# Queries of the second self attention by sets of seven products, with scores and transposes issued as one step

## The chip, the cores and the metric

The kernel runs on one core of a Trainium2 chip. A core has five engines that run side by side, each with an instruction queue of its own: TensorE (PE in the profile, with its weight loads as PEld), VectorE (DVE), ScalarE (ACT), GpSimd (POOL) and SyncE (SP), which here only issues DMA transfers. The metric is device time in microseconds (us) of one execution, and the time of a kernel is the median of its runs.

## The reference

A pre-LN decoder of two layers, all in float32, on x of 8 x 112 x 512 (8 sequences of 112 tokens, model width 512), with a context of 8 x 375 x 128. Each layer is

```
x = x + SelfAttention(LN(x))
x = x + CrossAttention(LN(x), context)
x = x + FFN(LN(x))
```

The two layers differ in kind. The part that matters here is the second layer's self attention: 16 heads of width 128 in four groups of four, each group with one key and one value head (grouped queries), rotary position on queries and keys, no bias, and a window mask of 128 positions that leaves out nothing at 112 tokens:

```
q = x @ Wq.T    (512 -> 16 heads x 128)      k, v = x @ Wk.T, x @ Wv.T   (512 -> 4 heads x 128)
q, k = q * cos + rotate_half(q) * sin, k * cos + rotate_half(k) * sin
out  = softmax(q k^T / sqrt(128)) v          then   x = x + out @ Wo.T
```

Ahead of it stands the first layer's FFN with ternary weights, behind it the second layer's cross attention and an FFN of experts.

## The kernel before

Tokens lie in 7 tiles of 128 (NT), and for the projections in two halves hf of 448 tokens (HT, four sequences). The normalised activations of a half, transposed, are xT[hf], 128 x 4 x 448. A float32 matmul shows in the trace as two PE instructions (passes).

**Turns.** The second self attention runs in eight turns (g, hf): group 0 with hf 0 and 1, then groups 1, 2, 3. A turn has two units of two sequences each. `prepare(n)` makes a turn's key and four query heads: `roped` (L621) multiplies with 4 matmuls of 128 x 448 (`accumulate`, L244), copies the result out of PSUM (raw_q or raw_k, L630 by VectorE; the first layer uses ScalarE at L632), starts two DMA transfers by SP that swap the halves of the head (turned_q, L637), multiplies raw by cos on GpSimd (L639) and turned by sin on VectorE (L640), and adds the two on GpSimd (L641). PSUM tiles of these products come from `mm`, which has two buffers.

**A unit.** `scores` (L695) gives eight 112 x 112 products; `softmax` takes the maximum on VectorE (nmax, L466), eight exponentials with sums on ScalarE (L469), a reciprocal on VectorE (L472) and the multiplication on GpSimd (L476). `probs_transposed` has two steps: four PE transposes each (ppt, L487) and a copy to pT (L488) by VectorE. `contexts` (L714) multiplies with the values and ScalarE copies the result to oT (L719).

**Outputs.** In groups 0 to 2 two token tiles at a time go through `out_pair`, which computes a 2 x 2 block product with seven block products instead of eight (`sevens`, L276 to L307, matmuls at L286). It needs sums of blocks: os (of oT) by `block_sums` (VectorE L253 and L257, GpSimd L256 and L258) and wos (of the weights) by `block_differences` (VectorE L267, L271, L272, GpSimd L270). After each product a *put* reads the PSUM bank: L771 copies, L768 adds, both on VectorE; x is completed by L782 and L785 on GpSimd. Several products accumulate on a bank that an earlier put has to read first. Single tiles go through `project_out` (L442, L446, L447).

**What sets the order.** `weave(main, filler)` lays filler steps between main steps in proportion to written costs. In `pipeline` (L493) the main steps of unit u of turn n are: scores of the following unit, the transposes of this one (0.45 each), its contexts; fillers are the next turn's `prepare` steps and the outputs, in proportion. Each engine's instructions then run in the order in which they were issued. The opening is at L1308: while the ternary FFN's last products (`fall`, L1245, with ScalarE top_h L1142 and VectorE rest_h L1143) run, `weave` inserts the first values, the tile normalisation of the coming attention (transposes `turned_tile`, L390 and copy L394) and the key and query steps of turn 0.

## Time and profile before

| what | value |
| --- | --- |
| runs shown | 1812.27, 1814.44, 1814.93 us (median 1814.44) |
| the profiled execution's own time | 1811.55 us |
| its span in the profile | 1809.5 us |
| mean granted TensorE clock | 0.998 of full speed |
| second self attention in the trace | about 884 to 1195 us of the span |
| in 884 to 1195 us: PE, VectorE, ScalarE, GpSimd busy | 305.2, 149.9, 66.2, 165.3 of 311 us |

The profile's page gives busy time of each engine, the chain of work that ended last, and groups of instructions by line. The trace behind it can be asked for one engine's waits, for the timeline of a stretch, or for busy time by windows with the granted clock. In a timeline row come the start in us, the duration in us, the engine, line and operation, out<-in, the shape, and in brackets the idle time before and what ended it.

### The profile page before, as it was taken

The page shows a single profiled execution, that of the slowest core. Times are in us where ns is not written, and L with a number is a line of the kernel's source. Part 1 is how long each engine was busy: PE and PEld are TensorE (multiplying, and loading weights), DVE is VectorE, ACT ScalarE, POOL GpSimd, SP SyncE. Part 2 cuts the span into 40 slices and gives each one's busy share as a digit, 9 for nine tenths or more (in the row PEclk, how much of TensorE's full clock was granted, in tenths as well). Part 3 has the DMA queues.
Part 4 walks back from the last instruction along what each step waited for, and adds up shares of the span by engine and source line. Part 5 has one row for each costly group of instructions (what it writes and reads, how often), then busy time and mean ns, then how long its engine had stood idle before and what let it go on. Part 6 is the DMA issues. An engine that isn't in the chain of part 4 may idle for free.

```text
span 1809.5 us, 20342 instructions
## 1 busy us (share of the span) xinstructions
PE 1762.9 (97%) x7150; PEld 989.6 (55%) x7150; DVE 952.1 (53%) x1692; ACT 627.8 (35%) x1906; POOL 770.7 (43%) x673
## 2 busy tenths in 40 slices
PE   8999999999999999999999999999999999999998
PEld 4455544555554555567655666655655444554444
DVE  4555666645353544786543555535765444444444
ACT  2444444554333433375321122136733111041110
POOL 3455555355555550000125666621363354434543
PEclk9999999999999999999999999999999999999999
DMA  6131422143233212011221221220011212011111
GB/s 243 27 119 54 151 82 75 75 152 110 53 79 108 59 53 93 24 71 47 76 60 36 82 73 41 44 86 1 2 44 50 73 62 81 24 51 55 63 34 41
DMA packets 40430, 124.50 MB, mean 69 GB/s; under 512 B 7333, under 2 KB 20701, under 8 KB 32905
## 3 DMA queue, kind: packets, MB, share of 16 engines
q1 hardware_dynamic: 33192, 93.73, 16.2%
q0 software_dynamic: 6848, 29.36, 5.4%
q8 instruction: 56, 0.92, 0.2%
q14 instruction: 46, 0.37, 0.1%
q10 hardware_dynamic: 288, 0.12, 0.0%
HBM read 94.56 MB, written 10.28 MB: 58 GB/s over the span
## 4 chain that ended last, share of the span: by engine, by line
PE 80%; DVE 8%; POOL 4%; DMA 3%; ACT 3%; issue 1%; SPq 1%; ACTq 0%; POOLq 0%; DVEq 0%
PE pr_q L244 10%; PE pf L244 5%; PE po_x L1004 4%; PE pb_dn L1550 4%; PE pv L244 3%; PE po_at L442 3%; PE ps L695 3%; PE po_at L446 3%; PE pr_k L244 3%; PE po_x L442 2%; PE po L714 2%; PE po_x L446 2%; PE pb_up L1550 2%; PE pa_dn L1550 2%; PE pq_x L244 2%; PE pg_dn L1550 2%
## 5 line engine op out<-in xcount | busy, mean ns | idle before, releaser
L244 PE MATMUL pr_q<-xT_at,wq 128*128 128x448 f32 x512 | 204.1, 543 | 0.0
L244 PEld LDWEIGHTS pr_q<-xT_at,wq 128*128 128x128 f32 x512 | 93.9, 190 | 84.3 <-issue 81.2
L469 ACT ACTIVATE p<-p,nmax 112x113 f32<-112x113 f32 x256 | 95.8, 376 | 109.7 <-DVE nmax L466 108.8
L476 POOL TENSOR_TENSOR p<-p,total 112x896 f32<-112x896 f32 (+1 forms) x56 | 85.3, 1529 | 94.9 <-DVE total L472 87.6
L1733 POOL TENSOR_TENSOR h<-silu,h 128x448 f32<-128x448 f32 x64 | 73.9, 1158 | 111.0 <-ACT silu L1731 110.8
L244 PE MATMUL pf<-h,sw 128*128 128x448 f32 x256 | 105.9, 540 | 0.0
L1127 POOL TENSOR_SCALAR tl<-tr,ternary_bounds 128x512 f32<-128x512 f32 x32 | 51.7, 1615 | 122.2 <-DMA tr<-in_c_w_dram 122.2
L974 DVE TENSOR_REDUCE nmax_x<-ps_x 112x2 f32<-112x750 f32 x64 | 57.2, 934 | 79.5 <-PE ps_x L968 79.5
L639 POOL TENSOR_TENSOR qT<-raw_q,tables 128x448 f32<-128x448 f32 x64 | 85.9, 1348 | 27.9 <-DVE raw_q L630 20.4
L641 POOL TENSOR_TENSOR qT<-qT,turned_q 128x448 f32<-128x448 f32 x64 | 75.5, 1183 | 50.4 <-DVE turned_q L640 41.6
L1735 DVE TENSOR_TENSOR h<-h,share 128x448 f32<-128x448 f32 x48 | 41.7, 875 | 105.0 <-POOL h L1733 105.0
L1004 PE MATMUL po_x<-pT_x,kv 125*128 125x448 f32 x192 | 89.2, 549 | 1.3 <-DVE pT_x L999 1.0
L976 ACT ACTIVATE p_x<-ps_x,nmax_x 112x375 f32<-112x375 f32 x124 | 69.7, 574 | 38.2 <-DVE nmax_x L974 38.1
L1550 PE MATMUL pb_dn<-h,sums_dn 128*128 128x448 f32 x192 | 80.2, 540 | 1.0 <-DVE xT_ff L1774 0.5
L1731 ACT ACTIVATE silu<-pf,cols 128x448 f32<-128x448 f32 x64 | 40.5, 633 | 115.6 <-PE pf L244 115.5
L488 DVE COPY pT<-ppt 112x448 f32<-112x448 f32 x96 | 57.1, 617 | 42.5 <-PE ppt L487 42.4
L469 ACT ACTIVATE p<-ps,nmax 112x112 f32<-112x112 f32 x128 | 43.2, 363 | 102.1 <-DVE nmax L466 102.1
L442 PE MATMUL po_at<-wo,oT 128*128 128x512 f32 x152 | 74.3, 611 | 0.0
L244 PEld LDWEIGHTS pf<-h,sw 128*128 128x128 f32 x256 | 48.5, 190 | 46.6 <-issue 40.5
L446 PE MATMUL po_at<-wo,oT 128*128 128x512 f32 x152 | 71.4, 592 | 0.0
L719 ACT COPY oT<-po 128x448 f32<-128x448 f32 x64 | 31.9, 525 | 104.8 <-PE po L714 104.8
L476 POOL TENSOR_TENSOR p_e<-p_e,total_e 112x896 f32<-112x896 f32 x16 | 26.9, 1682 | 96.5 <-DVE total_e L472 72.2
(357 smaller groups left out, 3942.5 us busy)
## 6 DMA issues: line engine op xcount, KB each, us to landing
tw<-in_c_w_dram SPq DMA_DIRECT2D x16, 512.0 KB
tr<-in_c_w_dram POOLq DMA_DIRECT2D x32, 256.0 KB, 3.9
signs<-tl POOLq DMA_DIRECT2D x32, 256.0 KB, 2.9
fup<-in_f_up_dram SPq DMA_DIRECT2D x8, 1024.0 KB
fdn<-in_f_dn_dram SPq DMA_DIRECT2D x8, 1024.0 KB
turned_q<-raw_q SPq DMA_DIRECT2D x128, 56.0 KB
turned_q<-raw_q SPq DMA_DIRECT2D x64, 112.0 KB
share<-gated SPq DMA_DIRECT2D x12, 448.0 KB
```

The source lines that it names most:

```text
L244: nc.tensor.matmul(ps, lhsT, rhs, start=(k == 0), stop=(k == len(pairs) - 1))
L442: nc.tensor.matmul(ps[0], lhsT, rhs, start=(c == 0), stop=False)
L446: nc.tensor.matmul(ps[0], lhsT, rhs, start=False, stop=(c == len(pairs) - 1))
L469: nc.scalar.activation(p[:, h, :], src[:, h, :], AF.Exp, bias=nmax[:, h : h + 1], accum_out=total[:, h : h + 1])
L476: spread[:] = [nc.gpsimd.tensor_tensor(p[:, at, :T], p[:, at, :T], total[:, at], ALU.mult).ins]
L639: nc.gpsimd.tensor_tensor(by_batch(dst), by_batch(raw), cos, ALU.mult)
L641: nc.gpsimd.tensor_tensor(dst, dst, turned, ALU.add)
L974: nc.vector.tensor_reduce(nmax, ps[:T, :, :L], AX.X, ALU.max, negate=True)
L976: e = nc.scalar.activation(p[:, 2 * j + s, :], ps[:T, s, :L], AF.Exp, bias=nmax[:, s : s + 1], accum_out=total[:, 2 * j + s : 2 * j + s + 1],)
L1004: nc.tensor.matmul(po[0][:, : 4 * T], kv[:, b, c, :], pTs[c], start=(c == 0), stop=(c == NLC - 1))
L1550: nc.tensor.matmul(bank[n], lhsT, rhs, start=(k == 0 and n in (1, 6, 7)), stop=(k == len(pairs) - 1), skip_group_check=True,)
L1733: nc.gpsimd.tensor_tensor(to, s, at["h1"][:, c, half(hf)], ALU.mult)
```

## The change

Six things change, all in the second layer's self attention.

1. In turns 2 to 7 the four query heads are computed as two pairs, each by `sevens` at 128 x 224: `paired`, with products of weight blocks (two heads wide, two halves of the model width) and token blocks (224 tokens). The sums of weight blocks come from `add_up(g)`, the differences of activation blocks from `differ(hf)`, laid among the steps of earlier turns. Six of seven puts of a pair are on VectorE, one on ScalarE.
2. The last addition of the rotation of the second pair's second query is on VectorE, the others stay on GpSimd.
3. Scores of the next unit and both transposes of this unit are issued as one main step of cost 2.1, so that no filler lies between.
4. The copy of the transposed probabilities is on ScalarE in this layer, and so are the raw copies of the keys and queries of turns 0 and 1.
5. The opening's `weave` lists keys and queries of turn 0 ahead of the second values step.
6. The temporaries os and od of `out_pair` come from the pool of normalised tiles (tag xn, three buffers), since the other pool now holds the sums.

The diff, cut to its core:

```diff
--- before.py
+++ after.py
@@ -476 +476 @@
             spread[:] = [nc.gpsimd.tensor_tensor(p[:, at, :T], p[:, at, :T], total[:, at], ALU.mult).ins]
         return p
 
-    def probs_transposed(pool, p, kept, name):
+    def probs_transposed(pool, p, kept, name, copy=nc.vector.tensor_copy):
 
 
         def turn(k):
@@ -485 +485 @@
             pt = turning(f"ppt_{name}_{k}").rearrange("p (h t) -> p h t", h=4)
             for h in range(4):
                 nc.tensor.transpose(pt[:T, h, :T], p()[:, 4 * k + h, :T], ident[:T, :T])
-            copied[:] = [nc.vector.tensor_copy(kept["pT"][:, 4 * k : 4 * k + 4, :], pt[:T, :, :T]).ins]
+            copied[:] = [copy(kept["pT"][:, 4 * k : 4 * k + 4, :], pt[:T, :, :T]).ins]
 
         return [(0.45, lambda: turn(0)), (0.45, lambda: turn(1))]
 
 
-    def pipeline(turns, units, ahead, prepare, scores, contexts, outputs, extra, begun=None, finale=None, between=False, keys_early=()):
+    def pipeline(turns, units, ahead, prepare, scores, contexts, outputs, extra, begun=None, finale=None, between=False, keys_early=(), grouped=False):
 
 
 
@@ -507 +507 @@
                 coming, own = scored(n * units + u + ahead), contexts(n, u)
                 if between:
                     steps += own[:2] + coming + own[2:]
+                elif grouped and coming:
+                    steps.append((2.1, lambda part=coming + own[:2]: run(part)))
+                    steps += own[2:]
                 else:
                     steps += coming + own
             return steps
@@ -548 +551 @@
         half = width // 2
         turns = [(g, hf) for g in range(G) for hf in range(2)]
         held, matrices = [{} for _ in turns], {}
-        dq, wos = [], {}
+        dq, xs, sums, wos = [], {}, {}, {}
 
...
@@ -606 +609 @@
             if n < 1:
 
                 first, last = (0, 3 if l0 else 2) if n < 0 else (6, 8)
-                return [(3.4, lambda b=b: values(b)) for b in range(first, last)]
+                steps = [(3.4, lambda b=b: values(b)) for b in range(first, last)]
+                if not l0 and n == 0:
+                    more = later(add_up(1) + differ(0))
+                    steps = [*more[:3], steps[0], *more[3:6], steps[1], *more[6:]]
+                return steps
             if not l0:
-                return []
+                g, hf = turns[n]
+                return later(differ(1) if n == 1 else add_up(g + 1) if hf == 0 and g + 1 < G else [])
...
+        def new_raw(name):
+            return top.tile([P, HT], F32, tag="raw", bufs=3, name=f"raw_{name}")
+
         def roped(dst, w, at, xh, bias, which, name):
+
+            ps = mm(f"pr_{name}")
+            accumulate(ps[:, :HT], [(w[:, c, at : at + P], xh[:, c, :]) for c in range(NC)])
+            raw = new_raw(name)
+            if bias is None and name.startswith("k") and xs:
+                nc.vector.tensor_copy(raw, ps[:, :HT])
+            elif bias is None:
+                nc.scalar.copy(raw, ps[:, :HT])
+            else:
+                nc.scalar.activation(raw, ps[:, :HT], AF.Identity, bias=bias)
+            rotated(dst, raw, which, name)
+
+        def differ(hf):
+
+            b = xT[hf].rearrange("p (h k) (s t) -> p h k s t", h=2, s=2)
+
+            def new():
+                xs[hf] = dq[0].tile([P, 4, 2, HT // 2], F32, tag=f"xs{hf}", bufs=1, name=f"xs_{layer}_{hf}")
+
+            return block_differences(
+                (nc.vector, nc.gpsimd), new, lambda k: xs[hf][:, k],
+                b[:, 0, :, 0], b[:, 0, :, 1], b[:, 1, :, 0], b[:, 1, :, 1],
+            )
+
+        def add_up(g):
+
+            a = matrices[g][0].rearrange("p (h k) (c m n) -> p h k c m n", h=2, c=2, m=2)
+
+            def new():
+                sums[g] = dq[0].tile([P, 3, 2, 2, P], F32, tag="sums", bufs=1, name=f"sums_{layer}_{g}")
+
+            return block_sums(
+                (nc.vector, nc.gpsimd), new, lambda k: sums[g][:, k],
+                a[:, 0, :, :, 0], a[:, 1, :, :, 0], a[:, 0, :, :, 1], a[:, 1, :, :, 1],
+            )
+
+        def paired(turn, qT, c, nm):
+
+            g, hf = turns[turn]
+
+            raw = [None, None]
+            half_ = HT // 2
+            tok = [slice(0, half_), slice(half_, HT)]
+
+            def products(n):
+                a = matrices[g][0].rearrange("p (h k) (c m n) -> p h k c m n", h=2, c=2, m=2)
+                b = xT[hf].rearrange("p (h k) (s t) -> p h k s t", h=2, s=2)
+                s, t = sums[g], xs[hf]
+                pick = {
+                    1: lambda k: (a[:, 0, k, c, 0], b[:, 0, k, 0]), 2: lambda k: (a[:, 1, k, c, 0], b[:, 1, k, 0]),
+                    3: lambda k: (s[:, 2, k, c], b[:, 1, k, 1]), 4: lambda k: (a[:, 1, k, c, 1], t[:, 3, k]),
+                    5: lambda k: (s[:, 0, k, c], t[:, 0, k]), 6: lambda k: (s[:, 1, k, c], t[:, 1, k]),
+                    7: lambda k: (a[:, 0, k, c, 1], t[:, 2, k]),
+                }
+                return [pick[n](k) for k in range(2)]
+
+            def put(n, ps):
+                if n == 1:
+                    raw[:] = [new_raw(f"q_{nm}_{2 * c + m}") for m in range(2)]
+                r0, r1 = raw
+                add = lambda to, of: nc.vector.tensor_tensor(to, of, ps, ALU.add)
+                if n == 1:
+                    nc.vector.tensor_copy(r0[:, tok[1]], ps)
+                elif n == 6:
+                    add(r1[:, tok[0]], r0[:, tok[1]])
+                elif n == 2:
+                    nc.scalar.copy(r0[:, tok[0]], ps)
+                elif n == 5:
+                    add(r1[:, tok[1]], r1[:, tok[0]])
+                elif n == 7:
+                    add(r1[:, tok[1]], r1[:, tok[1]])
+                elif n == 3:
+                    add(r0[:, tok[1]], r1[:, tok[0]])
+                    rotated(qT[:, 2 * c, :], r0, "q", f"q_{nm}_{2 * c}")
+                else:
+                    add(r1[:, tok[0]], r1[:, tok[0]])
+                    rotated(qT[:, 2 * c + 1, :], r1, "q", f"q_{nm}_{2 * c + 1}", nc.vector if c else nc.gpsimd)
+
+            first, second = sevens(products, put, half_, f"q_{nm}_{c}", c == 1)
+            return [(2.3, first), (3.0, second)]
+
+        def rotated(dst, raw, which, name, last=nc.gpsimd):
 
             cos, sin = (
                 const(f"{n}{which}{layer}").unsqueeze(1).to_broadcast([P, HB, T]) for n in ("cos", "sin")
             )
-            ps = mm(f"pr_{name}")
-            accumulate(ps[:, :HT], [(w[:, c, at : at + P], xh[:, c, :]) for c in range(NC)])
-            raw = top.tile([P, HT], F32, tag="raw", bufs=3, name=f"raw_{name}")
-            if bias is None:
-                nc.vector.tensor_copy(raw, ps[:, :HT])
-            else:
-                nc.scalar.activation(raw, ps[:, :HT], AF.Identity, bias=bias)
-
             turned = top.tile([P, HT], F32, tag="turned", bufs=3, name=f"turned_{name}")
             for at in range(0, P, half):
                 other = at ^ half
@@ -638 +723 @@
             by_batch = lambda t: t.rearrange("p (b t) -> p b t", b=HB)
             nc.gpsimd.tensor_tensor(by_batch(dst), by_batch(raw), cos, ALU.mult)
             nc.vector.tensor_tensor(by_batch(turned), by_batch(turned), sin, ALU.mult)
-            nc.gpsimd.tensor_tensor(dst, dst, turned, ALU.add)
+            last.tensor_tensor(dst, dst, turned, ALU.add)
 
...
-            more = later(lay(g - 1)) if not l0 and n and hf == 0 else []
-            for c in range(4):
-                steps += more[c : c + 1]
-                steps.append((3.0, lambda c=c: roped(
-                    qT[:, c, :], wq, c * P, xT[hf], col("bq", 4 * g + c) if l0 else None, "q",
-                    f"q_{nm}_{c}",
-                )))
+            if l0 or n < 2:
+                for c in range(4):
+                    steps.append((3.0, lambda c=c: roped(
+                        qT[:, c, :], wq, c * P, xT[hf], col("bq", 4 * g + c) if l0 else None, "q",
+                        f"q_{nm}_{c}",
+                    )))
+            else:
+                more = [step for c in range(2) for step in paired(n, qT, c, nm)]
+                if hf == 0:
+                    more = [step for pair in zip(more, later(lay(g - 1))) for step in pair]
+                steps += more
...
-            return probs_transposed(late, lambda: held[n]["p", u], kept, nm) + [(0.8 if l0 else 1.5, add, True)]
+            copy = nc.vector.tensor_copy if l0 else nc.scalar.copy
+            return probs_transposed(late, lambda: held[n]["p", u], kept, nm, copy) + [(0.8 if l0 else 1.5, add, True)]
 
...
@@ -742 +832 @@
 
             def add_up():
                 def new():
-                    s.append(dq[0].tile([P, 3, 2, P], F32, tag="os", bufs=1, name=f"os_{nm}"))
+                    pair = [npool.tile([P, D], F32, tag="xn", bufs=3, name=f"os_{nm}_{k}") for k in range(2)]
+                    d.append(pair[1][:, D // 2 :])
+                    pair = [t.rearrange("p (s c n) -> p s c n", s=2, c=2) for t in pair]
+                    s.extend([pair[0][:, 0], pair[0][:, 1], pair[1][:, 0]])
 
                 for step in block_sums(
-                    (nc.vector, nc.gpsimd), new, lambda k: s[0][:, k],
+                    (nc.vector, nc.gpsimd), new, lambda k: s[k],
                     a[:, 0, :, tok(0)], a[:, 1, :, tok(0)], a[:, 0, :, tok(1)], a[:, 1, :, tok(1)],
                 ):
                     step()
 
...
             def put(n, ps):
                 if n == 1:
-                    d.append(dq[0].tile([P, 3, D // 2], F32, tag="od", bufs=1, name=f"od_{nm}"))
-                d1, d2, d3 = (d[0][:, m] for m in range(3))
+                    d.append(npool.tile([P, D], F32, tag="xn", bufs=3, name=f"od_{nm}"))
+                d1, d2, d3 = d[0], d[1][:, : D // 2], d[1][:, D // 2 :]
...
+                        x[:, k + 1, :], x[:, k + 1, :], d[1], ALU.add
                     )
 
             first, second = sevens(products, put, D // 2, nm)
@@ -827 +920 @@
             pipeline(
                 turns, HB if l0 else HB // 2, 2 if l0 else 1, prepare, scores, contexts, outputs, extra,
                 begun=None if l0 else 0, finale=finale, between=l0,
-                keys_early=(2, 4) if l0 else (),
+                keys_early=(2, 4) if l0 else (), grouped=not l0,
             )
             if l0:
                 pool.release()
@@ -1305 +1398 @@
                     opening, following = self_attention(1, cross_attention_1, (nc.gpsimd, behind), xT)
 
             keys, values = opening[:5], opening[5:]
-            weave(main, values[:1] + third[1:] + values[1:] + keys[:-1] + more[:1] + keys[-1:] + more[1:])
+            weave(main, values[:1] + third[1:] + keys + more[:1] + values[1:] + more[1:])
             tpool.release()
             wpool2.release()
             following()
```

More of the change, by code (lines that the diff above doesn't have):

```diff
@@ L754, in products @@
                 b = matrices[g][1].rearrange("p (h k) (s n) -> p h k s n", h=2, s=2)
-                t, v = wos[g], s[0]
+                t, v = wos[g], s
                 pick = {
                     1: lambda c: (a[:, 0, c, tok(0)], b[:, 0, c, 0]), 2: lambda c: (a[:, 1, c, tok(0)], b[:, 1, c, 0]),
-                    3: lambda c: (v[:, 2, c], b[:, 1, c, 1]), 4: lambda c: (a[:, 1, c, tok(1)], t[:, 2, c]),
-                    5: lambda c: (v[:, 0, c], t[:, 0, c]), 6: lambda c: (v[:, 1, c], t[:, 1, c]),
+                    3: lambda c: (v[2][:, c], b[:, 1, c, 1]), 4: lambda c: (a[:, 1, c, tok(1)], t[:, 2, c]),
+                    5: lambda c: (v[0][:, c], t[:, 0, c]), 6: lambda c: (v[1][:, c], t[:, 1, c]),
                     7: lambda c: (a[:, 0, c, tok(1)], b[:, 0, c, 1]),
@@ L785, in put @@
                     nc.gpsimd.tensor_tensor(
-                        x[:, k + 1, :], x[:, k + 1, :], d[0][:, 1:].rearrange("p a b -> p (a b)"), ALU.add
+                        x[:, k + 1, :], x[:, k + 1, :], d[1], ALU.add
                     )
```

## Prediction

> **What bounds the kernel now.** I read the shares of busy time first, then the chain of work that ended last, then the waits of TensorE in the stretch of the second self attention (880 to 1215 us), then single stretches of its timeline. From the page of before, busy time and chain:
> ```profile
> PE 1762.9 (97%) x7150; PEld 989.6 (55%) x7150; DVE 952.1 (53%) x1692; ACT 627.8 (35%) x1906; POOL 770.7 (43%) x673
> ...
> PE 80%; DVE 8%; POOL 4%; DMA 3%; ACT 3%; issue 1%; SPq 1%; ACTq 0%; POOLq 0%; DVEq 0%
> ```
> PE is busy 97% and is 80% of the chain, so time goes with PE's passes and its idle gaps. Another engine counts only where PE waits for it. The waits of PE in that stretch (line, releaser, total, times, longest):
> ```profile
> PE ps L695 <- POOL qT L641: 2.3, 1, 2.3
> PE px_at_False L286 <- DVE od_at_False L771: 1.5, 3, 0.5
> ```
> One is the opening, the other recurs in the output sets of three turns. The rest of the list is below 1 us a line. So a gain must come from fewer passes, and a loss from new waits.
>
> **Passes removed.** Turns 2 to 7 compute four heads of queries. Before: 4 x 4 matmuls, which the trace shows as two passes each, 8 per head, 0.376 us from start to start at 448 wide: 32 passes, 12.03 us a turn. After: 2 pairs x 7 products x 2 x 2 passes = 56 passes at 224. No row has 224 wide; rows of 112 (scores, 16 passes in 1.57 us, 0.098 each) and of 256 bound it. The 256-wide sets, PE's timeline near 1004 us:
> ```profile
> 1003.74 1.03 PE L286 MATMUL py_at_True<-wo,os_at_True 128*128 128x256 f32 x4
> 1004.60 1.03 PE L286 MATMUL pz_at_True<-wos,oT 128*128 128x256 f32 x4
> ```
> First column start, second duration: 0.86 us for four passes, 0.216 each. Between 0.098 and 0.216 the line through both gives 0.190 at 224: 56 x 0.190 = 10.6 us, a gain of 1.42 a turn, **8.5 us over six turns**. Bounds: 0.216 gives 12.1 us and no gain; no reason is seen for less than 0.188, half of 0.376.
>
> **What the sets add around PE.** A product that accumulates into a bank starts only after the put of the earlier product has read it. The 256-wide put is 0.42 us and the 448 copy 0.62, so a 224 put is about 0.38; PE to DVE is about 0.2, DVE to PE 0.05. Four passes of 0.19 last 0.76, so one put fits (0.63), and a put with anything ahead of it on DVE does not. From the orders of both kernels:
> - raw_k's copy (0.62) is ahead of the first put: 0.13 a turn. The turned_k multiply (0.62) is ahead of a put of the first pair: 0.2.
> - Output set in front of the scores: turned_q3 and, in hf 0 turns, a sum of 0.44 stand ahead of a put: 0.33 (hf 1), 0.6 (hf 0). Output set behind the scores (hf 0 alone): two sums ahead of a put, 0.3 to 0.65, I take 0.45; but transposes now lie between its first products and the scores' maximum, which takes away that list's second row, 0.5 and 0.1 of unhidden weight load per turn.
> - hf 1: 0.2 for more puts beside sums of 512, and 0 to 0.4, taken 0.2, where the transposes follow scores directly and 7.3 us of work covers a chain of about 7.
>
> Sum: three hf 0 turns -1.42 + 0.13 + 0.2 + 0.6 + 0.45 - 0.62 = -0.66 each; hf 1 turns -1.42 + 0.13 + 0.2 + 0.33 + 0.2 + 0.2 = -0.36 twice, and -0.56 in the last, which has no sums. **Six turns: -3.3.** With no new stall it is -8.5 - 1.9 = -10.4; with 0.9 more a turn (below) +2.1.
>
> **Moved copies.** The transposed probabilities (DVE 0.61) go to ScalarE, where the like copy of oT is 0.53. 32 x 0.61 = 19.6 us leaves DVE, which gets 12 puts of 0.38 (4.6) for four copies of 0.62 (2.5) a turn, six turns: 12.4, and some twelve sums and differences of about 0.7, 8.4; eight raw query copies of turns 0 and 1 (5.0) leave it too. So DVE's load hardly moves. ScalarE's eight exponentials (2.8 us) may stand ahead of a copy; what covers it is the two to four products (over 2 us) between transposes and contexts. Cost 0; without cover about 1 us a unit. The last query add of each turn moves from GpSimd (1.14) to DVE, behind three puts: the chain from the last product to scores is 0.2 + 0.38 + 3.0 (a raw copy ends at 995.67, its turned multiply starts at 998.68) + 0.63 + 0.42 + 0.7 to 1.3 = 5.3 to 5.9, covered by the set of 7 x 0.865 = 6.05. Slack 0.1 to 0.8. The rotation's two SP issues per head stay as many; nothing is moved past them. The stores os and od only change pools: 0 (cover: three buffers).
>
> **The opening.** Keys and the first turn's queries are issued earlier, so that the last query has some 10 us of PE work behind it. PE and windows of before (sum columns: busy PE, load, DVE, ACT, POOL, granted clock, DMA share, GB/s):
> ```profile
> 926.43 1.34 PE L695 MATMUL ps<-kT,qT 128*112 128x112 f32 x12
> 930.07 3.84 PE L695 MATMUL ps<-kT,qT 128*112 128x112 f32 x20 [2.30 <-POOL qT L641]
> ```
> ```profile
> 930.00:932.00 2.00, 1.93 (x10) 1.93 (x11) 1.41 (x2) 0.09 (x1) 0.02 (x1) 0.54 0.00 0
> 932.00:934.00 2.00, 2.00 (x13) 1.93 (x12) 0.76 (x3) 1.71 (x11) 0.00 (x0) 0.61 0.04 8
> 934.00:936.00 2.00, 2.00 (x6) 0.81 (x5) 1.04 (x1) 2.00 (x13) 0.00 (x0) 1.00 0.00 0
> ```
> After an idle of 2.30 us the clock is 0.54 and 0.61, then 1.00: twenty passes took 3.84 instead of 20 x 0.098 = 1.97, so 1.87 more. The 2.30 + 1.87 = 4.17 go. But scores and both transposes are now one step, also in this first step, with nothing between: the transposes of unit 0 follow unit 1's scores (1.57 us). Before, value products (pv, 8 passes of 0.43, 3.4 us each) lay there. The chain of unit 0, timeline of VectorE, ScalarE and GpSimd of before:
> ```profile
> 931.16 1.09 DVE L466 TENSOR_REDUCE nmax<-ps 112x8 f32<-112x896 f32 x1 [0.59 <-PE ps L695]
> ...
> 938.26 3.32 POOL L476 TENSOR_TENSOR p<-p,total 112x896 f32<-112x896 f32 x2 [8.24 <-DVE total L472]
> ```
> 0.2 + 1.09 + eight exponentials 2.8 (932.29 to 935.07) + 0.1 + reciprocal 0.2 + half of 3.32, 1.66 + 0.1 = 6.2: idle 6.2 - 1.57 = 4.6 at least. In the new order VectorE has seven more operations between this maximum and its reciprocal (a sum of 512, unit 1's maximum 1.09, a tile's norm 0.54, two differences of 448, two of 512). The chain is then 1.3 + 0.66 + 1.09 + 0.54 + 4 x 0.66 + 0.2 + 1.76, some 8.2: idle 6.6. The trace has 1.33 and 1.32 us on average for such differences (L272, L271, 512 wide, 3 each), against 0.66 to 0.68 for the first; five at that price add 3.3: idle 9.9. I take 7.0, nearer the free row, since GpSimd is doing little there. The clock after so long an idle: 1.7 of extra time, between 0.9 and 2.6 (half and one and a half windows of the 3.4 us over which the record held 0.5). Opening: 7.0 + 1.7 - 4.17 = **+4.5** (from 4.6 + 0.9 - 4.17 = +1.3 to 9.9 + 2.6 - 4.17 = +8.3). ScalarE's copies of the raw queries, ahead of a step of the FFN that is still running, cost it +0.5 (0 to 1). The first wait in cross attention (pt_xa, 0.5) may go, since its DVE copy is no longer queued: -0.3.
>
> The Trainium skill, "TensorE: Matmul & The Clock Gate", section "Part 1: The HAM clock gate", says the clock falls to half after an idle window of about 3.4 us and returns after a busy one, and that these windows run free. By it the longer idle is certain to throttle, while the 2.30 us of the trace that did so would not alone fill a window; its sum is 3.4 x 0.5 = 1.7 of lost time, an estimate that leaves the opening at +4.5 too, and a stall under 1 us in the turns costs no clock. The skill also speaks against the change's order, "SBUF — State Buffer", section "Who interferes with whom": a VectorE operation with two SBUF inputs is locked out by a GpSimd one that reads SBUF. The rows agree in part (os sums of L257 took 0.42 us on average in some places and 0.83 in others). By this rule the upper end, idle 9.9, would hold, and the whole sum would be +4.3 instead of +1.4.
>
> **Sum.** +4.5 - 3.3 + 0.5 - 0.3 = +1.4 us. Against its own execution: 1811.55 (span 1809.5 and 2.05 around it, left as it is) becomes 1812.95. That execution is 2.9 under the median 1814.44 of the runs shown, which becomes **1815.8**.
>
> **Rivals.**
> (a) Full gain: puts hide, the unit 0 chain is as short as its rows. Six turns -7.5, opening +1.5, rest 0: -6, 1808.4. For it: DVE is only 53% busy. Against: puts are in order behind it.
> (b) Slower: DVE in order decides. If a rotation transfer lands so late that the turned multiply starts more than 3.0 us after its copy, the turned multiply holds the put behind it and PE waits in the products that accumulate; the first head's multiply has no slack beyond the contexts' 1.5 us, the last head's chain 0.1 to 0.8. From about 1 us of lateness it costs 0.9 a turn, 5.4 in all: 1821.2; the opening's upper end of +8.3, 3.8 above the value taken, gives 1819.6. For it: one such multiply in the trace waited 2.47 us for its DMA; the chain has DVE at 8%. Against: passes between are many.
> (c) The sets don't shorten the passes: at 0.216 a turn takes 12.1 instead of 10.6, 8.9 in all: 1824.7. Against: 0.098 at 112 wide, so weight loads don't set 0.19.
>
> **How the numbers follow.** The smallest difference that a measurement of this kernel can tell is about 0.2%, 3.6 us. Forecast 0.50 (1811 to 1818); (a) 0.14; (b) 0.31; (c) 0.05. The range takes the forecast, most of (a) and (b): 1809.5 to 1821.5. Faster takes (a), 0.14, and a rim of the forecast, 0.01; slower takes (b) without its lower rim, 0.29, with (c), 0.05: 0.34.
>
> **What would show it.** Right: the wait of scores for qT (2.3) gone, one wait of the transposes of unit 0 for GpSimd's probabilities of 5 to 10 us with a low clock after it; 224-wide passes at 0.19; waits of L286 on DVE puts of about 1 us a turn. Wrong: opening idle under 4 us, puts that hold PE over 2 us a turn, or a pass at 0.21.

## The result and the profile after

The changed kernel takes 1820.49 us (median of 5 runs, 1817.65 to 1822.79), the kernel before 1813.16 us over 5 runs: ratio 1.0041, 95% interval 1.0028 to 1.0054. That is slower by 7.3 us, 5.1 to 9.8 by the interval. The predicted 1815.8 was 4.7 us short, and as a difference it was 5.9 us short: +1.4 was forecast, +7.3 measured, since the three runs shown ahead of the prediction have a median 1.3 us above that of all five. The range to 1821.5 took the time in, but a difference within the noise was given the largest chance; slower, which came true, had 0.34.

Busy time and the head of the chain of the changed kernel, from its page:

```profile
PE 1761.9 (97%) x7294; PEld 1013.6 (56%) x7294; DVE 958.8 (53%) x1716; ACT 651.2 (36%) x1960; POOL 774.5 (43%) x675
...
PE 79%; DVE 9%; POOL 3%; ACT 3%; DMA 2%; issue 2%; SPq 1%; DVEq 0%; ACTq 0%; POOLq 0%
```

PE has 144 more passes, each shorter, and is busy 1.0 us less in a span that is 7.5 us longer. So most of the time was lost in gaps. The waits of PE in the stretch of the second self attention, 880 to 1225 us (line, releaser, total, times, longest):

```profile
PE ppt L487 <- POOL p L476: 7.7, 3, 7.4
PE pz_at_True L286 <- DVE od_at_True L861: 4.0, 6, 0.9
PE px_at_True L286 <- DVE os_at_True L864: 0.9, 2, 0.4
...
PE py_q L286 <- DVE raw_q L693: 0.7, 1, 0.7
```

The two rows shown of before are gone. In their place stand one long wait of the first transposes and many short ones of accumulating products for VectorE.

The same PE instruction can be looked up in both traces, so each stretch is a difference of two start times:

| stretch (both profiled executions) | before | after | difference |
| --- | --- | --- | --- |
| first value product to first scores | 49.92 | 50.18 | +0.3 |
| first scores to key of turn 1, with 0.77 of transposes that now lie ahead of this key taken off | 15.46 | 20.92 | **+5.5** |
| key of turn 1 to cross attention's first product, the 0.77 added | 252.35 | 254.04 | **+1.7** |
| on to the cross attention's first queries | 21.15 | 20.73 | -0.4 |
| from there to the end | 594.12 | 595.85 | +1.7 |

The start of the first row lies 1.2 us earlier after the change, before any changed step runs; with it the sum is the 7.5 us of the spans. The last row is no work of the change: there PE ran eight passes of the expert FFN in 4.89 us that took 3.25 before, since the granted clock was 0.50 from 1350 us on for 3.4 us.

**How large the waits are.** The profile's list leaves out short waits. I therefore also took, for each PE pass of the third row, its start-to-start interval less the free interval of its width (0.376 us at 448, 0.431 at 512, 0.216 at 256, 0.189 at 224, 0.098 at 112). The sum, called the excess here, is 3.4 us before and 13.7 after: 10.3 more, against 8.6 saved by shorter passes. That is the 1.7.

### The profile page after: what moved, and what is told of

It reads as the page before. It is cut to its first block, busy times and chain, and to the rows that moved or that the text cites. A ratio compares the mean times of both kernels' runs of the same rounds, so it can differ in the third digit from the quotient of the medians.

```text
span 1817.0 us, 20787 instructions
## 1 busy us (share of the span) xinstructions
PE 1761.9 (97%) x7294; PEld 1013.6 (56%) x7294; DVE 958.8 (53%) x1716; ACT 651.2 (36%) x1960; POOL 774.5 (43%) x675
## 4 chain that ended last, share of the span: by engine, by line
PE 79%; DVE 9%; POOL 3%; ACT 3%; DMA 2%; issue 2%; SPq 1%; DVEq 0%; ACTq 0%; POOLq 0%
PE pr_q L244 6%; PE pf L244 5%; PE po_x L1097 4%; PE pb_dn L1643 4%; PE po_at L442 3%; PE pv L244 3%; PE po_at L446 3%; PE pr_k L244 3%; PE pq_x L244 3%; PE po_x L442 2%; PE po_x L446 2%; PE pb_up L1643 2%; PE pa_dn L1643 2%; PE ps L784 2%; PE ps_x L1061 2%; PE po L803 2%
## 5 line engine op out<-in xcount | busy, mean ns | idle before, releaser
L244 PE MATMUL pr_q<-xT_at,wq 128*128 128x448 f32 x320 | 127.7, 545 | 0.0
L724 POOL TENSOR_TENSOR qT<-raw_q,tables 128x448 f32<-128x448 f32 x64 | 77.9, 1228 | 28.3 <-ACT raw_q L640 16.6
L244 PEld LDWEIGHTS pr_q<-xT_at,wq 128*128 128x128 f32 x320 | 58.7, 190 | 54.1 <-issue 50.5
L726 POOL TENSOR_TENSOR qT<-qT,turned_q 128x448 f32<-128x448 f32 x58 | 69.2, 1196 | 43.2 <-DVE turned_q L725 36.3
L725 DVE TENSOR_TENSOR turned_q<-turned_q,tables 128x448 f32<-128x448 f32 x64 | 51.8, 809 | 29.0 <-DMA turned_q<-raw_q 28.5
L1088 PEld LDWEIGHTS ppt_x<-consts,p_x 112*125 112x125 f32 x372 | 50.2, 188 | 29.6 <-issue 15.3
L784 PEld LDWEIGHTS ps<-kT,qT 64*112 64x112 f32 (+1 forms) x768 | 55.0, 175 | 13.8 <-issue 8.2
```

The lines of the kernel that those rows point to most:

```text
L244: nc.tensor.matmul(ps, lhsT, rhs, start=(k == 0), stop=(k == len(pairs) - 1))
L724: nc.gpsimd.tensor_tensor(by_batch(dst), by_batch(raw), cos, ALU.mult)
L726: last.tensor_tensor(dst, dst, turned, ALU.add)
L784: nc.tensor.matmul(ps[:T, 4 * k + h, :T], qT[at, h, bcols(b)], kT[at, bcols(b)], start=True, stop=True)
```

## The experiments

Diffs are cut to the lines that matter. Each time is a median beside runs of the kernel before on the same chip; since that one's median moved between 1811.5 and 1812.7 from one set of runs to the next, ratios are the better comparison. "Turns" is the third row of the table above, in the one profiled execution.

| kernel | median us | ratio to before (95%) | turns us | excess us |
| --- | --- | --- | --- | --- |
| before | 1813.16 | 1 | 252.4 | 3.4 |
| changed | 1820.49 | 1.0041 (1.0028 to 1.0054) | 254.0 | 13.7 |
| E1 opening split | 1811.39 | 0.9996 (0.9987 to 1.0005) | 254.0 | 13.6 |
| E2 nothing grouped | 1811.02 | 0.9992 (0.9983 to 1.0000) | 253.6 | 13.2 |
| E3 plain queries | 1807.42 | 0.9972 (0.9962 to 0.9982) | 250.3 | 1.3 |
| E4 late sums | 1811.37 | 0.9996 (0.9987 to 1.0005) | 253.9 | 13.6 |
| E5 early keys alone | 1808.72 | 0.9987 (0.9979 to 0.9996) | 252.3 | 3.4 |
| E6 plain, nothing grouped | 1807.03 | 0.9974 (0.9964 to 0.9984) | 250.1 | 1.1 |
| E7 rotation on GpSimd | 1818.11 | 1.0029 (1.0016 to 1.0042) | 263.3 | 22.9 |
| E8 additions left out | 1804.83 | 0.9961 (0.9950 to 0.9973) | 248.1 | 7.7 |
| E9 early keys, opening grouped | 1818.32 | 1.0037 (1.0023 to 1.0050) | 252.3 | 3.4 |
| E10 additions on VectorE | 1808.46 | 0.9981 (0.9972 to 0.9990) | 250.7 | 10.3 |
| E11 half of the sets | 1805.75 | 0.9967 (0.9955 to 0.9980) | 247.5 | 2.8 |
| E12 two od buffers | 1808.55 | 0.9980 (0.9970 to 0.9989) | 250.1 | 1.2 |

### E1: the opening split

```diff
-                elif grouped and coming:
+                elif grouped and coming and n:
```

> The changed kernel, but in turn 0 scores and transposes are separate main steps again, so that value products lie between them; all else of the change stays. Theory A (the opening's loss is this one grouping): the idle of 7.36 us ahead of the first transposes and about 2.1 us of half clock behind it go, and nothing replaces them, since three value and key products of over 10 us cover a chain of some 10 us: about 9.5 us under the changed kernel, 1811 us. Rival B (the probabilities are late wherever the transposes stand, because sums of weights and activations stand ahead of them on VectorE and GpSimd): the wait shrinks by the products put in between, but 2 to 4 us of idle stay, and with them the low clock: 1815 us. Rival C: the old wait of scores for the rotated query comes back: 1816 us.

Measured 1811.39 us, 9.1 under the changed kernel: theory A. The opening of the changed kernel, PE and then GpSimd:

```profile
925.51 3.31 PE L784 MATMUL ps<-kT,qT 128*112 128x112 f32 x32
936.18 1.74 PE L487 MATMUL ppt<-consts,p 112*112 112x112 f32 x8 [7.36 <-POOL p L476]
937.71 8.37 PE L244 MATMUL pv<-wv,xT_at 128*112 128x512 f32 x16
```

```profile
929.26 4.77 POOL L258 TENSOR_TENSOR sums<-wq,sums 128x512 f32<-128x512 f32 x1 [0.63 <-DVE sums L257]
934.00 3.77 POOL L476 TENSOR_TENSOR p<-p,total 112x896 f32<-112x896 f32 x2
```

All 32 score passes run through in 3.31 us, so the old wait for the rotated query is gone. Then PE stands for 7.36 us, and eight transposes and two value products take some 2.1 us more than at full clock (9.74 us up to the next transposes, against 7.7 at the free intervals above). The windows show it (granted clock is the third number from the end):

```profile
936.00:938.00 2.00, 1.82 (x9) 1.82 (x10) 0.00 (x0) 0.58 (x2) 1.76 (x2) 0.50 0.04 8
938.00:940.00 2.00, 2.00 (x3) 0.65 (x3) 0.00 (x0) 0.49 (x1) 0.00 (x0) 0.50 0.00 0
940.00:942.00 2.00, 2.00 (x5) 0.77 (x4) 0.00 (x0) 0.00 (x0) 0.00 (x0) 0.90 0.00 0
```

With value and key products in between (E1) no wait of the first transposes is left. The excess of the turns stays: the opening and the turns are two losses.

### E2 and E3: grouping or sets

```diff
-                keys_early=(2, 4) if l0 else (), grouped=not l0,
+                keys_early=(2, 4) if l0 else (), grouped=False,
```

> The changed kernel with scores and both transposes as separate main steps in all turns. Theory A (grouping hurts only in the opening; the waits of the turns come from additions that stand ahead of puts on VectorE): within 2 us of the kernel split in turn 0 alone, with the waits of the output sets on VectorE still some 1 us a turn and 0.5 us more in three turns where the transposes no longer lie between an output set's first products. Rival B (grouping packs the work on VectorE and ScalarE into bursts, and makes the waits of the turns): 4 us or more under the kernel split in turn 0 alone.

```diff
-            if l0 or n < 2:
+            if True:
...
-                    more = later(add_up(1) + differ(0))
...
-            if bias is None and name.startswith("k") and xs:
+            if bias is None and name[4] != "0":
```

> As the kernel split in turn 0 alone, but all queries by plain products of 448 and without the sums and differences that only the sets use; raw copies of groups 1 to 3 by VectorE as before the change, transposed probabilities by ScalarE and scores grouped with transposes from turn 1 on. Theory A (the sets save 8.5 us of passes, and their puts and sums bring about as much in waits): within 3 us of the kernel split in turn 0, with the waits of the output sets on VectorE nearly gone. Rival B (the waits come from grouping, from ScalarE's copies or from the pools, and the sets themselves gain): 6 to 9 us over the kernel split in turn 0, with the waits unchanged.

E2 is 0.4 under E1 with overlapping intervals, its excess 13.2: no gain or loss by grouping in the turns is seen. Theory A held, but for the 0.5 us more in three turns, which didn't come (E12 below has the reason). E3 is 4.0 under E1 and its excess 1.3: A's reason held, no wait of the output sets is listed, but A had allowed 3 us. The sets save 8.6 us of passes and bring 12.3 us of waits: they lose 3.7 (254.0 less 250.3).

### E4: late sums

```diff
+        def after_puts(step):
+            with tc.issue_after(last_put[0]) if last_put else nullcontext():
+                step()
...
-                    step()
+                    after_puts(step)
```

> As the kernel split in turn 0 alone, but VectorE issues the sums of oT blocks and of query weight blocks only after the last put of the output set that stands before them in the program. Theory A (those sums, lengthened by GpSimd to 1.3 us each, hold the puts that PE waits for): the waits of the fourth and seventh product of the output sets fall from 1.0 and 1.2 us a turn to under 0.4, 4 to 6 us in all: 1805 to 1807 us, faster than both kernels. Rival B (the turned queries that wait for their transfers hold the puts, and the sums only stand beside them): less than 2 us: 1809 to 1811 us.

Neither gain came: 1811.37 us, excess 13.6. The waits moved: in hf 0 turns the wait of the set's last product fell from 0.87 to 0.53, and that of the third product, 0.45 in two hf 1 turns, went, but the sums then stood ahead of the scores' maximum, and PE met the result there:

```profile
1045.69 1.83 PE L788 MATMUL ps<-kT,qT 128*112 128x112 f32 x16 [1.00 <-ACT p L469]
1047.92 0.98 PE L487 MATMUL ppt<-consts,p 112*112 112x112 f32 x8 [0.40 <-POOL p L476]
```

The time is B's. Theory A as I put it, that these sums alone hold the puts, fell.

### E8 and E10: standstill or queue

```diff
-                    rotated(qT[:, 2 * c, :], r0, "q", f"q_{nm}_{2 * c}")
+                    rotated(qT[:, 2 * c, :], r0, "q", f"q_{nm}_{2 * c}", None)
...
-                    rotated(qT[:, 2 * c + 1, :], r1, "q", f"q_{nm}_{2 * c + 1}", nc.vector if c else nc.gpsimd)
+                    rotated(qT[:, 2 * c + 1, :], r1, "q", f"q_{nm}_{2 * c + 1}", nc.vector if c else None)
```

> As the changed kernel split in turn 0, but GpSimd's last addition of the rotation is left out for the queries of the sets (so three of four query heads of a turn lack their sine part); the additions of VectorE stay. Theory A (a VectorE operation with two SBUF inputs stands still while one of GpSimd's runs: the sum of oT blocks of 1.30 us and the second turned query of 1.2 to 1.5 us do so): both fall to their free durations of 0.44 and 0.62; the wait of the seventh product in the three output sets of hf 0 falls from 0.87 to under 0.3 us, the sum by 3 to 5 us: 1806 to 1809 us. Rival B (these durations have another reason, such as the transfers that land beside them): they stay, and the time within 1 us of 1811.4.

1804.83 us, 1.2 below theory A's range and far from B's. VectorE in an hf 0 turn of E1 (first, with the row of GpSimd's addition beside it) and of E8 (second), at the same place in the output set; the addition on GpSimd is missing in E8:

```profile
999.70 0.41 DVE L861 TENSOR_TENSOR od_at_True<-od_at_True,py_at_True 128x256 f32<-128x256 f32 x1
1000.02 1.30 DVE L253 TENSOR_TENSOR os_at_False<-oT 128x256 f32<-128x256 f32 x1
1001.25 0.61 DVE L725 TENSOR_TENSOR turned_q<-turned_q,tables 128x448 f32<-128x448 f32 x1
1001.78 0.41 DVE L861 TENSOR_TENSOR od_at_True<-od_at_True,pz_at_True 128x256 f32<-128x256 f32 x1
...
999.91 1.13 POOL L726 TENSOR_TENSOR qT<-qT,turned_q 128x448 f32<-128x448 f32 x1 [1.68 <-DVE turned_q L725]
```

```profile
998.43 0.41 DVE L862 TENSOR_TENSOR od_at_True<-od_at_True,py_at_True 128x256 f32<-128x256 f32 x1
998.76 0.42 DVE L253 TENSOR_TENSOR os_at_False<-oT 128x256 f32<-128x256 f32 x1
999.10 0.62 DVE L725 TENSOR_TENSOR turned_q<-turned_q,tables 128x448 f32<-128x448 f32 x1
999.63 0.41 DVE L862 TENSOR_TENSOR od_at_True<-od_at_True,pz_at_True 128x256 f32<-128x256 f32 x1
```

The sum of oT blocks takes 1.30 us beside GpSimd's addition and 0.42 without it; the put behind it (last row) starts 2.08 us after the row above the sum, against 1.20. PE waits for that put: 0.87 in E1, and no wait is listed in E8. The puts themselves, with one operand in PSUM, take 0.41 in both.

By place, of the 5.9 us of excess that E8 takes away 2.6 lie in the output sets of the hf 0 turns (1.14 to 0.26 a turn), 1.7 in the second pairs, 0.4 in the last turn's output set, and 1.1 where transposes follow the scores at the end of two hf 1 turns; that last part is no put: there the transposes no longer wait for GpSimd's probabilities. In the output sets of those two hf 1 turns, the ones with sums of weight blocks, nothing went: 1.6 us a turn in E1 and in E8. There a sum and a turned query still take 1.33 and 1.35 in E8, each beside another operation of GpSimd, a multiplication by cos and GpSimd's own part of the sums (VectorE, then GpSimd):

```profile
1030.11 1.33 DVE L257 TENSOR_TENSOR sums<-sums,wq 128x512 f32<-128x512 f32 x1
1034.40 1.35 DVE L725 TENSOR_TENSOR turned_q<-turned_q,tables 128x448 f32<-128x448 f32 x1
...
1029.44 1.45 POOL L724 TENSOR_TENSOR qT<-raw_q,tables 128x448 f32<-128x448 f32 x1 [5.11 <-DVE raw_q L693]
1033.62 1.65 POOL L258 TENSOR_TENSOR sums<-wq,sums 128x512 f32<-128x512 f32 x1
```

So theory A holds where the addition runs beside VectorE's operation, and its forecast for the turned query fails here, where the neighbour is another. That these neighbours are the cause in the hf 1 turns is read from the rows; no run left them out.

```diff
-                    rotated(qT[:, 2 * c, :], r0, "q", f"q_{nm}_{2 * c}")
+                    rotated(qT[:, 2 * c, :], r0, "q", f"q_{nm}_{2 * c}", nc.vector)
...
-                    rotated(qT[:, 2 * c + 1, :], r1, "q", f"q_{nm}_{2 * c + 1}", nc.vector if c else nc.gpsimd)
+                    rotated(qT[:, 2 * c + 1, :], r1, "q", f"q_{nm}_{2 * c + 1}", nc.vector)
```

> As the changed kernel split in turn 0, with the last addition of the rotation on VectorE for all queries of the sets, nothing left out. Theory A (two things hold the puts: VectorE's queue, and the standstill beside GpSimd): the second turned query falls from 1.2 to 1.5 us to 0.62, but 0.62 of addition stands in its place, so the waits shift and hardly shrink: 1809 to 1813 us. Rival B (the standstill alone makes the waits): 1804 to 1807 us, as with the additions left out.

1808.46 us lies between the two expectations. Within the self attention the turned queries fell from a mean of 0.80 us (changed kernel) to 0.63, the excess from 13.6 (E1) to 10.3. Both causes are real: of the 12.3 us of waits that the sets bring, 5.9 go when GpSimd's additions are left out (E8), and 3.3 of these remain gained when VectorE does them, so that the additions cost 2.6 again on VectorE. Part of these is queue, seen in the hf 0 turns, where the rows nearly have their free durations and 0.46 us a turn are left, against 0.26 in E8; part is a standstill once more, since in two hf 1 turns one of the additions takes 1.35.

### E7: rotation on GpSimd

In the sets `by` and `last` are GpSimd, elsewhere they stay.

```diff
-            nc.vector.tensor_tensor(by_batch(turned), by_batch(turned), sin, ALU.mult)
+            by.tensor_tensor(by_batch(turned), by_batch(turned), sin, ALU.mult)
```

> As the changed kernel split in turn 0, but in the sets GpSimd does the multiplication of the turned query by the sine and all last additions, so VectorE has none of the rotation of these queries. Theory A (VectorE's rotation work stands ahead of puts, and is held by GpSimd's additions on top): the waits of L286 for VectorE fall from about 10 us in all to under 4; scores wait for GpSimd's last addition, whose chain grows to about 7.4 us behind a cover of 6.05, by some 1.3 us a turn: between 1806 and 1811 us. Rival B (the puts themselves, one behind another, make the waits): they stay within 2 us of what they were, 1811 to 1819 us.

1818.11 us: the time is B's, and the waits of L286 for VectorE hardly fell, to 4.6 us from the 5.6 that the profile lists for E1 (I had counted the hidden ones in). But they are not what made the time; the new wait of scores for GpSimd was larger than I had worked out:

```profile
PE ps L784 <- POOL qT L726: 6.1, 4, 2.4
```

and the clock was at half for 6.8 and 3.4 us within the turns; with both the excess rose to 22.9. So E7 doesn't tell the two theories apart.

### E5, E9 and E12: the other parts one by one

E5 is the kernel before with the opening's order alone:

```diff
-            weave(main, values[:1] + third[1:] + values[1:] + keys[:-1] + more[:1] + keys[-1:] + more[1:])
+            weave(main, values[:1] + third[1:] + keys + more[:1] + values[1:] + more[1:])
```

> The kernel before the change with one edit: the opening lists keys and queries of turn 0 ahead of the second values step. Theory A (of the change's parts this one alone takes away the opening's wait of scores for the rotated query, 2.30 us, and 1.87 us of half clock behind it): 4.2 us under the kernel before, 1808.3 us. Rival B (the wait goes only together with other parts, or the time comes back in the ternary FFN that runs beside it, whose split parts now queue behind copies of queries): under 1.5 us.

In its trace, first scores to key of turn 1 takes 11.28 us instead of 15.46: the 4.2 are gone. The median shows 2.7 (ratio 0.9987, 0.9979 to 0.9996), which rules out A's full 4.2 in the runs' times and leaves B's figure open there; its runs' granted clocks lie between 0.995 and 0.998 (see the end).

E9 adds to E5 the grouping of turn 0:

```diff
+                elif units == HB // 2 and not n and coming:
+                    steps.append((2.1, lambda part=coming + own[:2]: run(part)))
+                    steps += own[2:]
```

> The kernel before with early keys and queries, plain queries and VectorE's copies, and scores grouped with the transposes in turn 0 alone. Theory A (the opening's idle is the chain from maximum to probabilities, and the sums and differences that the sets add on VectorE and GpSimd lengthen it): PE waits for the first probabilities 4.6 to 6.5 us instead of 7.36, with 1.7 to 2.6 us of half clock behind it: 6 to 9 us over the kernel with early keys alone, 1815 to 1817.5 us. Rival B (the chain does not see the added sums): the idle is 7.2 to 7.5 us, 1818 us.

```profile
934.02 1.70 PE L487 MATMUL ppt<-consts,p 112*112 112x112 f32 x8 [4.70 <-POOL p L476]
```

The idle is 4.70 us, as A had it; 1818.32 us is B's time. In the profiled execution the opening costs 4.70 + 1.9 over E5; the median is 3 us worse than that execution would give, with three of five runs at a granted clock of 0.996 and two at 0.993 and 0.992; where those lost it stays open. What is shown is the idle: the chain alone makes 4.7, and the changed kernel has 2.7 more. That the sets' sums in the queues make these is read from the changed kernel's rows (GpSimd's sum of 4.77 us above); E9 has neither the sets nor ScalarE's copies.

E12 adds to E5 a second buffer:

```diff
-                    d.append(dq[0].tile([P, 3, D // 2], F32, tag="od", bufs=1, name=f"od_{nm}"))
+                    d.append(dq[0].tile([P, 3, D // 2], F32, tag="od", bufs=2, name=f"od_{nm}"))
```

> The kernel before with early keys and queries and one more edit: the temporary od of the output sets has two buffers instead of one; nothing grouped, no sets of queries, copies of the transposed probabilities on VectorE. Theory A (the wait of 0.52 us in the output sets behind the scores, and the 0.16 and 0.10 us beside it, come from the single buffer, which GpSimd's addition of x still reads; the change took it away by its move of os and od into another pool): the wait is gone, 2.2 us under the kernel with early keys alone, 1806.5 us, as the plain kernel without grouping. Rival B (the move of the copies to ScalarE took it away, by leaving VectorE free): the wait stays and so does 1808.7 us.

The wait is gone and the turns take 250.1 us as in E6, with all copies still on VectorE: theory A. The cause can be read in the kernel before, GpSimd first, then VectorE:

```profile
1007.68 1.26 POOL L785 TENSOR_TENSOR x<-x,od_at_True 128x512 f32<-128x512 f32 x1
```

```profile
1008.98 0.42 DVE L771 COPY od_at_False<-px_at_False 128x256 f32<-128x256 f32 x1 [0.65 <-PE py_at_False L286]
```

The copy into the new od starts 0.04 us after GpSimd has read the old one. The profile names PE as releaser, though PE had long been done. The median, 1808.55, is B's and that of E5; by ratios it is 0.9980 against 0.9987, whose intervals overlap, so the 2.2 us are shown in the trace and not in the times.

### E6 and E11: what is worth keeping

> Plain queries of 448 in all turns, no sets, no grouping in any turn; ScalarE copies of the transposed probabilities and the early keys stay. Theory A (grouping and the copies on ScalarE are worth about 2 us together, by the wait of the output set behind the scores, 0.68 and 0.10 us in three turns): within 2.5 us of the plain kernel that groups, 1807 to 1810 us. Rival B (grouping alone makes the plain kernel fast): 4 us over it, 1811.5 us.

E6 (E2 and E3 together) is 1807.03 us with an excess of 1.1: A.

```diff
...
-                more = [step for c in range(2) for step in paired(n, qT, c, nm)]
+                more = paired(n, qT, 0, nm) + [(3.0, lambda c=c: roped(
+                    qT[:, c, :], wq, c * P, xT[hf], None, "q", f"q_{nm}_{c}",
+                )) for c in (2, 3)]
...
```

> Nothing grouped, early keys and ScalarE's copies as in the changed kernel; the first two query heads of turns 2 to 7 by one set of seven, the other two by plain products with raw copies on ScalarE; sums of weight blocks for these heads alone, half as long. Theory A (the waits come from the second pair, whose puts meet the turned queries of the first, and from the output set that follows it; the first pair costs some 0.4 us a turn of the 0.71 that it saves): 1805 to 1807.5 us, at or under the plain kernel without grouping (1807.0). Rival B (a set's two turned queries, that come 0.76 us apart, and the sums cost as much wherever the set stands): 1808.5 to 1811 us.

1805.75 us, ratio 0.9967 (0.9955 to 0.9980): the fastest version that computes everything, 6 us under the kernel before and 14.7 under the changed one by medians. Excess 2.8: one set per turn costs some 0.3 us, at its first puts, and hardly more. I put that down to the plain heads behind it, which leave 3 us of passes per copy; the sums are also half as long here, and no run parts the two. Its interval overlaps E6's, so that it beats E6 is shown by the trace (247.5 against 250.1 us), not by the times.

## Why the prediction was right and wrong

**Passes: right.** 224 wide is 0.189 us; predicted 0.190, gain 8.5, measured 8.6. Rival (c) fell.

**Opening: right, with one wrong reason.** Predicted idle 7.0, clock 1.7, net +4.5; measured 7.36, 2.1, +5.5 (0.2 more around them). I took the lower row "since GpSimd is doing little there". VectorE's operations did keep their free durations of 0.6 to 0.7 us, but GpSimd's sum took 4.77, against 1.65 for its operation of the same size just before, and the probabilities had to wait for it until 934.00, 1.0 us after the reciprocal. The size came out near all the same, by luck in part. E1 and E9 show the rest: the grouping makes it, and 4.7 us are the bare chain.

**Turns: wrong, and this is the step that failed.** Predicted -3.3, measured +1.7. By place, excess after the change against the terms of the sum:

| place, all six turns | predicted us | measured us |
| --- | --- | --- |
| first put behind the key's copy | 0.8 | 1.3 |
| turned key ahead of a put | 1.2 | 0.7 |
| second pair, behind the turned queries of the first | 0.4 (for sums; the pair itself was given nothing) | 2.5 |
| output set ahead of the scores | 1.8 (hf 0) + 1.0 (hf 1) | 3.4 + 4.0 |
| output set behind the scores, against 2.3 before | 1.35 | 0.5 |
| scores and transposes at the end of hf 1 turns | 0.6 | 1.1 |

The term that failed is the output set ahead of the scores (0.33 and 0.6 a turn; 1.3 and 1.1 measured). I priced each operation ahead of a put at its free row, 0.44 for a sum and 0.62 for a turned query, and kept the longer rows for the range. In the hf 0 turns the sum lasts 1.30, because the two query heads of a pair are finished 0.76 us apart and GpSimd's addition for one runs just when VectorE has the sum; in the second pair, which I had given no wait of its own, it meets the next turned query (0.85 to 1.17). E8 shows this by taking the addition away. In the two hf 1 turns with sums of weight blocks the rows of 1.33 and 1.35 lie beside other operations of GpSimd instead; E8 leaves their 1.6 us a turn as they are. E4 takes the first half of it away (its sums come later, and the third product's wait goes), but loses as much elsewhere. E10 shows that VectorE's queue counts beside the standstill (0.46 a turn with nearly free rows). The prediction's own sign of being wrong, puts that hold PE over 2 us a turn, is just met by the excess at puts (some 12.4 us in six turns), while the profile's list has 5.6 us.

Rival (b) had the mechanism of VectorE in order, and its size (+5.4; the turns were 5.0 over the forecast), but not its cause. A late transfer shows in one turn alone: in the first hf 1 turn with sets the first head's multiply starts 3.70 us after its put, against 2.99 and 3.07 in the hf 0 turns beside it, and the second pair's excess is 0.9 instead of 0.2 to 0.3. So that the range, which had (b)'s price for its upper end, took the measured time in was luck.

**The wait in the output set behind the scores: near in size, wrong in cause.** I took away 0.62 a turn, 1.9 in all, because transposes lie in between; 2.3 went. E2 loses the wait without that grouping, and E5 and E12 show that the pool did it, which I had priced at 0.

**ScalarE's copies:** 0 was right (E6 against E12: 250.1 us both). The cross attention's 0.3 was 0.4. **The clock** outside the opening was in no term: +1.7 in the profiled execution.

The Trainium skill, "SBUF — State Buffer", section "Who interferes with whom", has the rule that decided: a VectorE operation with two SBUF inputs contends with a GpSimd one that reads SBUF, one with at most one SBUF input does not. E8's rows agree (1.30 against 0.42; the puts, which read their other input from PSUM, 0.41 throughout). I had applied it to the opening alone, and there the measurement differs from my reading of it: the idle was 7.36, not 9.9, since GpSimd's sum stood and VectorE's operations mostly did not.

## What to carry to other kernels

Price an operation ahead of a wait by what will run on the neighbouring engine when it gets there, not by its free row: a change that makes two results ready close together, or lays sums on both engines, can move VectorE and GpSimd onto each other. Shorter passes leave less time per put, so work that PE used to hide comes into view; use the cheaper algorithm only as far as the engine behind it has room (half of the sets beat all of them by the times, and none by the trace). A single buffer can be the true releaser where the profile names an engine that was long done.

## What the runs showed of the hardware

VectorE and GpSimd don't slow each other evenly. In the opening, GpSimd's addition of 512 that started at 929.26 took 4.77 us, while four of VectorE's operations with two SBUF inputs that started after it kept 0.61 to 0.68; only the fifth stood:

```profile
930.56 0.61 DVE L271 TENSOR_TENSOR xs<-xT_at,xs 128x448 f32<-128x448 f32 x1
931.09 0.68 DVE L267 TENSOR_TENSOR wos<-wo 128x512 f32<-128x512 f32 x1
931.70 0.61 DVE L272 TENSOR_TENSOR xs<-xT_at,xs 128x448 f32<-128x448 f32 x1
932.23 0.68 DVE L271 TENSOR_TENSOR wos<-wo,wos 128x512 f32<-128x512 f32 x1
...
932.95 1.63 DVE L272 TENSOR_TENSOR wos<-wo,wos 128x512 f32<-128x512 f32 x1
```

In the turns it was VectorE that stood.

The granted clock fell also where PE was not idle. Changed kernel, expert FFN, behind 24 passes of only 8 columns:

```profile
1347.45 2.81 PE L244 MATMUL pgate<-wg,xT_ff 128*128 128x8 f32 x24
1350.11 4.89 PE L244 MATMUL pf<-xT_ff,fup 128*128 128x448 f32 x8
```

```profile
1348.00:1350.00 2.00, 2.00 (x20) 2.00 (x19) 1.59 (x2) 0.38 (x1) 1.92 (x2) 1.00 0.00 0
1350.00:1352.00 2.00, 2.00 (x5) 1.18 (x5) 2.00 (x2) 0.00 (x0) 2.00 (x2) 0.50 0.00 0
```

The kernel before went through the same place in its profiled execution at full clock:

```profile
1341.64 2.74 PE L244 MATMUL pgate<-wg,xT_ff 128*128 128x8 f32 x24
1344.24 3.25 PE L244 MATMUL pf<-xT_ff,fup 128*128 128x448 f32 x8
```

Ten of the twelve experiments' profiled executions had such a stretch of 3.4 us there. What decides it from one execution to the next isn't settled. One such stretch costs 1.6 us here, and the five runs of one kernel spread by 2.7 us (before) and 5.1 (changed), as large as the effects looked for; that the clock makes this spread wasn't shown.
